# ScalarE fetches some token rows beside SyncE, and offsets are read 32 at a time

## The chip, the cores and the metric

The program runs on one core of one Trainium2 chip. A core has a matrix engine (TensorE, PE in the profile), two vector-like engines (VectorE, DVE; ScalarE, ACT), a general engine (GpSimd, POOL) and SyncE (SP), which only issues DMAs. Each has its own queue of instructions, worked through in order, and they wait for each other through semaphores. DMAs can be issued from SP, ACT and POOL. The metric is the device time of one execution in microseconds (us), lower being better; the median of three runs counts. One further execution was recorded by the hardware profiler, and all durations below come from that one.

## The reference

A batch of 16384 rows goes through a recommender network:

```python
tok = word_emb[token_idx].mean(axis=1)          # 32 tokens of a 50000 x 300 table
e1, e2, e3 = (emb_mh[k][mh_idx[k]].mean(axis=1) for k in (1, 2, 3))   # 20 indices each, 64 wide
o1, o2, o3, o4 = (emb_oh[k][oh_idx[k]] for k in (1, 2, 3, 4))         # one index each
emb = concatenate([tok, e1, e2, e3, o1, o2, o3, o4], axis=1)          # 748 wide
wide = sums of one weight per small index
h = relu(emb @ W1 + b1); h = relu(h @ W2 + b2); h = relu(h @ W3 + b3) # 1024, 512, 256
return sigmoid(h @ Wd + bd + wide)
```

What matters here is the first line: 16384 x 32 rows of 300 float32 (1200 bytes) are picked out of a table in HBM and added up, 32 for each batch row.

## The kernel before, in words

**Tiles.** The batch is cut into 128 tiles of 128 rows; a batch row lies on a partition.

**The tokens.** `tokens()` (L289 to L312) works through the tiles in groups of two tokens (`TOK_GROUP`). A token of a tile is one indirect DMA issued from POOL (L303): it reads 128 indices, one a partition, and fetches 128 rows of the table. Six buffers of two tokens (`TOK_BUFS`) are in rotation, and `add_up` (L275 to L287) adds a group into a running sum on DVE three groups later (L279, L281, L286). The 32nd token (`j == N_TOK - 1`) of some tiles is not gathered by POOL: if the tile stands in `fetched`, its rows are there already and the group has one indirect DMA fewer.

**The fetches.** Which tiles those are is set by the list `fetches`: tiles from 4 on with `t % 5` equal to 0, 2 or 4. For each, `load_column` (L317 to L322) loads the tile's 128 indices of that token into one partition with a DMA from SP, `column_offsets` (L324 to L330) turns them into byte offsets with two small DVE operations, and `fetch` (L332 to L350) reads the offsets into SP's registers, 16 at a time (`LOADS`, one TENSOR_LOAD, L338), and issues one DMA of 1200 bytes for each row from SP (L347). The rows go to one of two buffers of the pool `fetched`. A fetch is spread over 20 steps (`FETCH_STEPS`) and starts 24 steps (`FETCH_AHEAD`) before the step in which the tile's last group is added up; its column is loaded 4 steps ahead of that and converted 1 step ahead.

**The small tables.** The other embeddings are turned into products: for six batch rows a step, DVE makes one-hot vectors of the indices (`hot`, L406), ACT scales a part of them (L413), PE multiplies them to counts (`pc`, L424), ACT copies the counts out (`cnt`, L427), and a tile later PE multiplies the counts with the tables (`pg`, L459) and DVE adds the parts up (`g`, L449). The tables are split into three bfloat16 terms first (`convert_tables`), with the small constants `minus_count` and `zeros`, which nothing reads later.

**The layers.** Of three tiles together, PE transposes the features (L500), DVE copies them out (`x`, L504), PE runs the layers in float32 (L577, outputs L609), and ACT applies bias and ReLU (`h`, L588). SP stores the results (L621).

**The order.** The order on each engine is written out by hand: a loop over 1435 steps (11 a tile and 27 at the end) calls each of these pieces in turn, and each engine's queue holds them in that order. `tokens_by` gives how many groups the token stream should have made by a step (2 a step for 24 steps, then an even pace). Within a step the order is: one-hots and the scaling for the next step, eviction of earlier layer outputs, counts and their eviction, small sums, transposes, column loads and offsets, the rows of the fetches under way, the token groups, key columns, the layers, late small sums. `speed` sets how much of the layers is done in a step: one tile in 10.4 steps, in 8.5 near the end and in 6.0 (`TILE_STEPS_LAST`) in the last 14 steps. `load_indices` (L352 to L369) loads the indices of two tiles from SP: one DMA for the tokens (L357) and two for the small tables (L362).

**Semaphores of DMAs.** DMAs issued from SP and ACT share eight semaphores in rotation, in the order in which the program is written, and each DMA waits until the DMA eight before it, which had its semaphore, has landed. POOL's indirect DMAs have eight of their own.

Of the kernel before, what the change touches and what calls it, by code (L numbers as in the profile page):

```python
# [19 lines left out]
P = 128  # L20
N_TOK, TOK_D = 32, 300
N_MH, EMB = 20, 64
ROW = EMB + 1
# [3 lines left out]
TOK_BUFS = 6  # L27
HOT_BUFS = 2
FETCH_FROM = 4
FETCH_STEPS = 20  # L30
FETCH_AHEAD = 24
COLUMN_AHEAD = 4
COLUMN_LAG = 1
LOADS = 16
ROW_BYTES = 4 * TOK_D
WAKE = 27
EARLY = 3
BLOCK = 256
# [4 lines left out]
FRONT_PACE = 2.0  # L43
TILE_STEPS = 10.4
TILE_STEPS_SUMS = 8.5
TILE_STEPS_LAST = 6.0
STORE_LAG = 2
HALF = P // 2
UPPER = 256.0
# [23 lines left out]
IDX_MH = N_TOK  # L73
IDX_COLS = N_TOK + N_SMALL
# [3 lines left out]
def kernel(  # L78
# [21 lines left out]
    nc = tc.nc  # L100
    B = out.shape[0]
    NSUB, N = BLOCK // P, LAYER_TILES * P
# [5 lines left out]
    for f in SMALL:  # L108
        n = -(-tables[f].shape[0] // P)
# [4 lines left out]
    const = ctx.enter_context(tc.tile_pool(name="const", bufs=1))  # L114
# [3 lines left out]
    ohp = ctx.enter_context(tc.tile_pool(name="onehot", bufs=HOT_BUFS))  # L118
    cp = ctx.enter_context(tc.tile_pool(name="counts", bufs=2))
    fp = ctx.enter_context(tc.tile_pool(name="fetched", bufs=2))  # L120
    gp = ctx.enter_context(tc.tile_pool(name="g", bufs=3))
    wp = ctx.enter_context(tc.tile_pool(name="wide", bufs=2))
    xp = ctx.enter_context(tc.tile_pool(name="x", bufs=1))
# [51 lines left out]
    at = 0  # L175
# [2 lines left out]
        at += n  # L178

    terms = const.tile([P, n_h, 3 * ROW], BF16, name="terms")  # L180
    minus_count = const.tile([P, P], BF16, name="minus_count")
    nc.vector.tensor_single_scalar(minus_count, ident, -1.0 / COUNT, op=ALU.mult)

    zeros = const.tile([P, ROW], F32, name="zeros")
    nc.vector.memset(zeros, 0.0)

    def load_tables(part0, tag):
# [100 lines left out]
    def tokens():  # L288

        under_way = []  # L290
        for n in range(n_all):
            if n < n_all - TOK_LAG:
                t, q = divmod(n, n_groups)
                it = token_indices[t // NSUB][:, t % NSUB, :].bitcast(U32)
                tok_rows = tokp.tile([P, TOK_GROUP * TOK_D], F32, name="tok_rows")
                rows = []
                for r in range(TOK_GROUP):
                    j = q * TOK_GROUP + r
                    if j == N_TOK - 1 and t in fetched:
                        rows.append(fetched.pop(t))  # L300
                        continue
                    rows.append(tok_rows[:, r * TOK_D : (r + 1) * TOK_D])
                    nc.gpsimd.indirect_dma_start(  # L303
                        out=rows[-1],
                        out_offset=None,
                        in_=word,
                        in_offset=bass.IndirectOffsetOnAxis(ap=it[:, j : j + 1], axis=0),
                    )
                under_way.append((t, q, rows))
            if n >= TOK_LAG:  # L310
                add_up(*under_way.pop(0))
            yield 1  # L312

    fetched, columns = {}, {}
    word_bytes = word.bitcast(U8).rearrange("n d -> (n d)").unsqueeze(0)

    def load_column(t):  # L317

        columns[t] = fp.tile([1, P], I32, name="column")
        nc.sync.dma_start(  # L320
            out=columns[t], in_=idx[t * P : (t + 1) * P, N_TOK - 1 : N_TOK].rearrange("n o -> o n")
        )  # L322

    def column_offsets(t):  # L324


        column = columns[t]
        low = ROW_BYTES & -ROW_BYTES
        nc.vector.tensor_single_scalar(column, column, ROW_BYTES // low, op=ALU.mult)
        nc.vector.tensor_single_scalar(column, column, low.bit_length() - 1, op=ALU.logical_shift_left)  # L330

    def fetch(t):  # L332


        rows = fp.tile([P, TOK_D], F32, name="fetched").bitcast(U8)
        column = columns.pop(t)
        for p0 in range(0, P, LOADS):
            _, values = nc.values_load_multi_w_load_instructions(  # L338
                column[:, p0 : p0 + LOADS],
                engines=[mybir.EngineType.SP],  # L340
                min_val=0,
                max_val=(word.shape[0] - 1) * ROW_BYTES,
                skip_runtime_bounds_check_because="the indices are rows of the table",
            )
            for i, value in enumerate(values):
                p = p0 + i
                nc.sync.dma_start(out=rows[p : p + 1, :], in_=word_bytes[:, bass.ds(value, ROW_BYTES)])  # L347
                if p == P - 1:
                    fetched[t] = rows.bitcast(F32)
# [323 lines left out]
    tiles = B // P  # L673
# [40 lines left out]
    ix = load_indices(0)  # L714
# [8 lines left out]
    for step in range(n_steps):  # L723
        t, i = divmod(step, STEPS)
        s = t % NSUB
# [40 lines left out]
        for at, t_f in fetches:  # L766
            if step == at - COLUMN_AHEAD:
                load_column(t_f)
            if step == at - COLUMN_LAG:
                column_offsets(t_f)  # L770
            if step == at:
                fetching.append((at, Paced(fetch(t_f))))
        for at, rows in list(fetching):
            rows.to(P * (step + 1 - at) / FETCH_STEPS)
            if step + 1 - at >= FETCH_STEPS:
                rows.finish()
                fetching.remove((at, rows))
# [78 lines left out]
```

## Time and profile before

| what | value |
|---|---|
| time, median of three runs | 7247.27 us (7244.57 to 7274.91) |
| time of the profiled execution | 5068.49 us |
| its span, first to last instruction | 5066.7 us |
| mean granted TensorE clock | 0.982 |
| busy PE, DVE, ACT, POOL | 4811.1, 3748.8, 2739.9, 3807.6 us |
| indirect DMAs from POOL | 4021 |
| rows fetched by SP one by one | 9600 (75 tiles) |
| bytes moved by DMA | 653.52 MB, of these 617.88 MB by POOL's queue |

The span begins with the first instruction of the program and ends with the last; 1.8 us lie around it in the profiled execution. "Busy" counts the time in which an engine works on an instruction; issuing a DMA from SP or ACT, reading registers and waiting for semaphores are the sequencer's work and not in it. For POOL an indirect DMA is in it[...]. Of a line of the list of groups, the numbers after the bar are the busy time in all, the mean of one in ns, and the idle time of the engine just ahead of such instructions with what ended it. In the view of a tile's instructions the three numbers are the shortest, the median and the longest in ns, followed by the first and the last start in us. The time of the runs without the profiler is 1.43 times that of the profiled execution; the profile doesn't tell where the other 2178.8 us are.

### The profile page before, as it was taken

Reading aid. Unit: us, or ns where it says so; the run is one execution under the profiler, and the core shown is the slowest. Engines: PE = TensorE matmul, PEld = TensorE weight load, DVE = VectorE, ACT = ScalarE, POOL = GpSimd, SP = SyncE. Lnnn points to the kernel's source line nnn. Section 1 sums busy time; section 2 is a strip of 40 time slices with the busy share of each in tenths; the row PEclk is TensorE's granted clock in tenths of the full one; section 3 lists DMA queues with packets and bytes.
Section 4 is the critical chain, followed back from the end, with each engine's and each line's share of the span. In section 5 each row is a group of like instructions: output and inputs, shape, how many; then the busy total and the mean of one; then the engine's idle time right before and its main releaser. Section 6 shows DMA issues by size and latency. Waiting matters only on the chain.

```text
span 5066.7 us, 115364 instructions
## 1 busy us (share of the span) xinstructions
PE 4811.1 (95%) x36252; PEld 3731.2 (74%) x36252; DVE 3748.8 (74%) x6814; ACT 2739.9 (54%) x3658; POOL 3807.6 (75%) x4028
## 2 busy tenths in 40 slices
PE   6799999999999999999999999999999999999998
PEld 4577776677776777677777777767767888888898
DVE  6777777777777777777777777777777777777773
ACT  5455555555555555555555555555555555555552
POOL 7777777777777777777777777777777777777775
PEclk9899999999999999999999999999999999999999
DMA  7444444444444444444444444444444444444443
GB/s 203 127 128 128 128 128 128 128 128 128 127 128 129 127 128 128 128 129 127 128 128 127 128 128 126 128 129 127 128 128 127 128 129 128 128 128 127 129 127 97
DMA packets 280720, 653.52 MB, mean 129 GB/s; under 512 B 139419, under 2 KB 149659, under 8 KB 280103
## 3 DMA queue, kind: packets, MB, share of 16 engines
q0 software_dynamic: 193008, 617.88, 45.3%
q1 hardware_dynamic: 87095, 28.26, 2.7%
q8 instruction: 283, 4.64, 0.4%
q14 instruction: 334, 2.74, 0.2%
HBM read 645.63 MB, written 0.07 MB: 127 GB/s over the span
## 4 chain that ended last, share of the span: by engine, by line
PE 58%; DMA 14%; DVE 11%; issue 8%; POOL 4%; SPq 2%; ACT 1%; DVEq 0%; POOLq 0%; ACTq 0%
PE ph L577 31%; PE pg L459 20%; DMA tok_rows<-in_word_emb_dram,it 14%; PE pc L424 6%; POOL tok_rows L303 4%; DVE hot L406 4%; DVE own L286 3%; DVE own L281 2%; SPq L347 2%; PE pc L500 1%; DVE x L504 1%; ACT hot L413 1%; DVE g L449 1%; SPq L338 1%; ACT cnt L427 0%
## 5 line engine op out<-in xcount | busy, mean ns | idle before, releaser
L303 POOL DMA_INDIRECT tok_rows<-in_word_emb_dram,it x4021 | 3806.7, 947 | 1226.9 <-issue 784.0
L413 ACT ACTIVATE hot<-hot 64x768 bf16<-64x768 bf16 (+1 forms) x1408 | 1155.5, 821 | 1728.6 <-DVE hot L406 1717.0
L459 PE MATMUL pg<-terms,cnt 128*128 128x195 bf16 x17664 | 1723.6, 249 | 35.5 <-DVE g L449 35.5
L459 PEld LDWEIGHTS <-cnt 128*128 128x128 fp8e3 x17664 | 1529.0, 98 | 107.0 <-issue 80.1
L577 PE MATMUL ph<-x,w_sb 128*128 128x384 f32 (+5 forms) x4932 | 1506.4, 444 | 63.7 <-DVE x L504 53.6
L406 DVE TENSOR_TENSOR hot<-own,sc 128x1656 bf16<-128x1656 bf16 (+1 forms) x1408 | 1394.3, 990 | 213.3 <-PE pc L424 134.9
L427 ACT ACTIVATE cnt<-pc 128x828 uint16<-128x828 f32 (+1 forms) x1408 | 1187.5, 843 | 385.7 <-PE pc L424 367.5
L577 PE MATMUL ph<-h,w_sb 128*128 128x384 f32 (+2 forms) x4160 | 1221.7, 434 | 1.5 <-ACT h L588 1.5
L286 DVE TENSOR_TENSOR own<-own,tok_rows 128x300 f32<-128x300 f32 x1792 | 857.2, 478 | 377.2 <-DMA tok_rows<-in_word_emb_dram,it 327.2
L577 PEld LDWEIGHTS ph<-x,w_sb 128*128 128x128 f32 (+1 forms) x4932 | 846.1, 194 | 374.6 <-DVE x L504 62.9
L281 DVE TENSOR_TENSOR own<-own,tok_rows 128x300 f32<-128x300 f32 x1920 | 917.5, 478 | 233.5 <-DMA tok_rows<-in_word_emb_dram,it 178.3
L424 PEld LDWEIGHTS <-hot 128*128 128x128 bf16 x8192 | 592.5, 98 | 465.0 <-issue 201.0
L577 PEld LDWEIGHTS ph<-h,w_sb 128*128 128x128 f32 x4160 | 700.9, 191 | 250.5 <-ACT h L588 3.7
L424 PE MATMUL pc<-hot 128*128 128x138 bf16 x8192 | 729.5, 225 | 90.8 <-ACT hot L413 81.4
L588 ACT ACTIVATE h<-ph,b_sb 128x384 f32<-128x384 f32 (+2 forms) x723 | 379.1, 524 | 140.3 <-PE ph L577 125.6
L449 DVE TENSOR_REDUCE g<-pg 128x130 f32<-128x390 f32 (+1 forms) x512 | 259.8, 507 | 238.8 <-PE pg L459 236.7
L504 DVE TENSOR_TENSOR x<-pc,scale 128x768 f32<-128x768 f32 x127 | 120.9, 952 | 49.8 <-PE pc L500 49.0
L500 PE MATMUL pc<-ident,g 128*128 128x128 f32 x762 | 108.0, 279 | 9.8 <-ACT cnt L427 8.9
L393 DVE COPY sc<-pc 128x512 bf16<-128x512 bf16 x64 | 44.1, 689 | 81.5 <-PE pc L389 79.5
L279 DVE TENSOR_TENSOR own<-tok_rows 128x300 f32<-128x300 f32 x128 | 61.4, 480 | 47.2 <-DMA tok_rows<-in_word_emb_dram,it 44.2
L500 PEld LDWEIGHTS pc<-ident,g 128*128 128x128 f32 x762 | 84.1, 143 | 15.5 <-ACT cnt L427 14.3
L609 PE MATMUL po<-h,wd_sb 128*1 128x384 f32 (+2 forms) x208 | 70.6, 426 | 21.9 <-ACT h L588 20.7
(56 smaller groups left out, 436.6 us busy)
## 6 DMA issues: line engine op xcount, KB each, us to landing
fetched<-in_word_emb_dram SPq DMA_DIRECT2D x9600, 1.2 KB
tok_rows<-in_word_emb_dram,it POOLq DMA_INDIRECT x4021
ix<-in_idx_dram SPq DMA_DIRECT2D x128, 32.0 KB
w_sb<-in_W_dram SPq DMA_DIRECT2D x6, 512.0 KB
raw<-in_mh_dram SPq DMA_DIRECT2D x4, 682.5 KB
it<-in_idx_dram SPq DMA_DIRECT2D x64, 32.0 KB
w_sb<-in_W_dram SPq DMA_DIRECT2D x1, 2048.0 KB
column<-in_idx_dram SPq DMA_DIRECT2D x75, 0.5 KB
```

Of the source, the lines that this page charges most:

```text
L281: nc.vector.tensor_add(tok_sum, tok_sum, a)
L286: nc.vector.tensor_add(to, tok_sum, b)
L303: nc.gpsimd.indirect_dma_start(out=rows[-1], out_offset=None, in_=word, in_offset=bass.IndirectOffsetOnAxis(ap=it[:, j : j + 1], axis=0),)
L406: nc.vector.tensor_tensor(hot[:, 0 : 2 * rows, :].rearrange("p i (n d) -> p i n d", d=2), iota.rearrange("p (n d) -> p n d", d=2).unsqueez ...
L413: nc.scalar.activation(upper, upper, AF.Copy, scale=UPPER)
L424: nc.tensor.matmul(pc[:, k // n, at : at + n_h], hot[:, 2 * k, 0:P], hot[:, 2 * k + 1, :], start=True, stop=True)
L427: nc.scalar.activation(cnt[:, :, b : b + rows].rearrange("l h (g k) -> l h g k", g=2), pc[:, :, 0 : n * n_h].rearrange("l g (k h) -> l h g ...
L449: nc.vector.tensor_reduce(field_columns(features(t), pair), pg[:, 0:n, :].rearrange("p f (c d) -> p f d c", c=3), AX.X, ALU.add,)
L459: nc.tensor.matmul(pg[:, j, :], by_slice[:, h, :], terms[:, h, :], start=(h == h0), stop=(h == h1 - 1))
L500: nc.tensor.transpose(pt[:, j // n, j % n, :], g[:, c : c + P], ident)
L577: nc.tensor.matmul(to, weights[: src.shape[0], k, m * P : (m + 1) * P], src, start=(k == 0), stop=(k == len(srcs) - 1),)
L588: nc.scalar.activation(dst[:, m, 0:n], ph[:, 0:n], AF.Relu, bias=bias[:, m : m + 1])
```

## The change

SP now fetches the 32nd token of tiles from 4 on with `t % 3` equal to 1 or 2, spread over 16.5 steps that start 25 or 19.5 steps ahead. ACT fetches the 31st token (`N_TOK - 2`) of every fourth tile from tile 8 on, in the same manner, over 38 steps that start 42 steps ahead. TENSOR_LOADs read 32 offsets each instead of 16. ACT's rows have one buffer, in a new pool; the column of its offsets lies where `minus_count` and `zeros` were, in a common tile `early_use`. `load_indices` loads the small indices of two tiles with one DMA instead of two. In the last 14 steps the layers are done at one tile in 9 steps instead of 6. Line numbers of the new kernel are up to 5 higher in `tokens` and the groups after it, so that L303 becomes L308, L347 becomes L356, and L338 becomes L347.

```diff
-FETCH_STEPS = 20
-FETCH_AHEAD = 24
+FETCH_STEPS = 16.5
+FETCH_AHEAD = {1: 25.0, 2: 19.5}
+SCALAR_FROM, SCALAR_EVERY = 8, 4
+SCALAR_STEPS = 38.0
+SCALAR_AHEAD = 42.0
-LOADS = 16
+LOADS = 32
-TILE_STEPS_LAST = 6.0
+TILE_STEPS_LAST = 9.0
...
+    fa = ctx.enter_context(tc.tile_pool(name="fetched_scalar", bufs=1))
...
-    minus_count = const.tile([P, P], BF16, name="minus_count")
+    early_use = const.tile([P, P // 2 + ROW], I32, name="early_use")
+    minus_count = early_use[:, 0 : P // 2].bitcast(BF16)
...
-    zeros = const.tile([P, ROW], F32, name="zeros")
+    zeros = early_use[:, P // 2 : P // 2 + ROW].bitcast(F32)
...
-                    if j == N_TOK - 1 and t in fetched:
-                        rows.append(fetched.pop(t))
+                    if (t, j) in fetched:
+                        rows.append(fetched.pop((t, j)))
...
-    def load_column(t):
-        columns[t] = fp.tile([1, P], I32, name="column")
+    def load_column(t, j):
+        columns[t, j] = early_use[0:1, 0:P] if j < N_TOK - 1 else fp.tile([1, P], I32, name="column")
...
-    def fetch(t):
-        rows = fp.tile([P, TOK_D], F32, name="fetched").bitcast(U8)
-        column = columns.pop(t)
+    def fetch(t, j):
+        by_scalar = j < N_TOK - 1
+        rows = (fa if by_scalar else fp).tile([P, TOK_D], F32, name="fetched").bitcast(U8)
+        column = columns.pop((t, j))
+        queue, engine = (
+            (nc.scalar, mybir.EngineType.Activation) if by_scalar else (nc.sync, mybir.EngineType.SP)
+        )
         for p0 in range(0, P, LOADS):
...
-                engines=[mybir.EngineType.SP],
+                engines=[engine],
...
-                nc.sync.dma_start(out=rows[p : p + 1, :], in_=word_bytes[:, bass.ds(value, ROW_BYTES)])
+                queue.dma_start(out=rows[p : p + 1, :], in_=word_bytes[:, bass.ds(value, ROW_BYTES)])
...
-        for s in range(NSUB):
-            nc.sync.dma_start(
-                out=ix[s * HALF : (s + 1) * HALF],
-                in_=idx[b0 + s * P : b0 + (s + 1) * P, IDX_MH:IDX_COLS].rearrange(
-                    "(p f) c -> p f c", f=2
-                ),
-            )
+        nc.sync.dma_start(
+            out=ix, in_=idx[b0 : b0 + BLOCK, IDX_MH:IDX_COLS].rearrange("(p f) c -> p f c", f=2)
+        )
...
-    fetches = [(int(summed_at(t)) - FETCH_AHEAD, t) for t in range(FETCH_FROM, tiles) if t % 5 % 2 == 0]
+    fetches = [
+        (summed_at(t) - FETCH_AHEAD[t % 3], FETCH_STEPS, t, N_TOK - 1)
+        for t in range(FETCH_FROM, tiles)
+        if t % 3
+    ]
+    fetches += [
+        (summed_at(t) - SCALAR_AHEAD, SCALAR_STEPS, t, N_TOK - 2)
+        for t in range(SCALAR_FROM, tiles, SCALAR_EVERY)
+    ]
...
+        for at, n, *of in fetches:
+            if step == int(at) - COLUMN_AHEAD:
+                load_column(*of)
+            if step == int(at) - COLUMN_LAG:
+                column_offsets(*of)
+            if step == int(at):
+                fetching.append((at, n, Paced(fetch(*of))))
+        for entry in list(fetching):
+            at, n, rows = entry
+            rows.to(P * (step + 1 - at) / n)
+            if step + 1 - at >= n:
+                rows.finish()
+                fetching.remove(entry)
```

More of the change, by code (lines that the diff above doesn't have):

```diff
@@ L315, with column_offsets @@
     word_bytes = word.bitcast(U8).rearrange("n d -> (n d)").unsqueeze(0)
-    def load_column(t):
-        columns[t] = fp.tile([1, P], I32, name="column")
+    def load_column(t, j):
+        columns[t, j] = early_use[0:1, 0:P] if j < N_TOK - 1 else fp.tile([1, P], I32, name="column")
         nc.sync.dma_start(
-            out=columns[t], in_=idx[t * P : (t + 1) * P, N_TOK - 1 : N_TOK].rearrange("n o -> o n")
+            out=columns[t, j], in_=idx[t * P : (t + 1) * P, j : j + 1].rearrange("n o -> o n")
         )
-    def column_offsets(t):
-        column = columns[t]
+    def column_offsets(t, j):
+        column = columns[t, j]
         low = ROW_BYTES & -ROW_BYTES
@@ L346, in fetch @@
                 p = p0 + i
-                nc.sync.dma_start(out=rows[p : p + 1, :], in_=word_bytes[:, bass.ds(value, ROW_BYTES)])
+                queue.dma_start(out=rows[p : p + 1, :], in_=word_bytes[:, bass.ds(value, ROW_BYTES)])
                 if p == P - 1:
-                    fetched[t] = rows.bitcast(F32)
+                    fetched[t, j] = rows.bitcast(F32)
                 yield 1
@@ L765 @@
             layers, target = start(block), 0
[L766 to L775, printed above, removed]
+        for at, n, *of in fetches:
[9 more added lines that the diff above has]
+            if step + 1 - at >= n:
                 rows.finish()
-                fetching.remove((at, rows))
+                fetching.remove(entry)
         toks.to(tokens_by(step + 1))
```

## The prediction

> **What bounds the kernel now.** I read the groups of the page first, then the instructions of the token tile, then the waits, then a long stretch in the middle.
>
> ```profile
> PE 4811.1 (95%) x36252; PEld 3731.2 (74%) x36252; DVE 3748.8 (74%) x6814; ACT 2739.9 (54%) x3658; POOL 3807.6 (75%) x4028
> ...
> q0 software_dynamic: 193008, 617.88, 45.3%
> q1 hardware_dynamic: 87095, 28.26, 2.7%
> ```
>
> By busy time PE looks like the bound (95%) and POOL far from it (75%). The next view, the instructions of the token tile, says otherwise:
>
> ```profile
> L303 POOL DMA_INDIRECT tok_rows<-in_word_emb_dram,it x4021: 942/946/1372, 3.0 to 5034.2; - x192
> ```
>
> The 4021 gathers start between 3.0 and 5034.2 us, so they follow each other every 5031.2 / 4020 = 1.2515 us on average, while one takes 0.946 us. What lies between two of them is in the waits:
>
> ```profile
> POOL tok_rows L303 <- issue: 784.0, 2572, 0.3
> ...
> DVE own L286 <- DMA tok_rows<-in_word_emb_dram,it: 327.2, 509, 2.9
> ...
> DVE own L281 <- DMA tok_rows<-in_word_emb_dram,it: 178.3, 247, 3.1
> ...
> PEld L424 <- ACT hot L413: 115.6, 92, 5.2
> PE pc L424 <- ACT hot L413: 81.4, 60, 4.5
> ```
>
> POOL's longest gap is 0.3 us, the same as its mean (784.0 / 2572): a fixed price of one gather, not a wait for anybody. In the trace's records only 25 of the 4020 distances are over 1.3 us, and these add 4.6 us together. So POOL never waits for a buffer, for indices or for another engine, from the first gather to the last, and the adders on DVE wait for it. The stretch from 1000 to 4000 us (us, then busy time of PE, PEld, DVE, ACT and POOL) shows how close PE follows:
>
> ```profile
> 1000.00:4000.00 3000.00, 2888.89 (x21144) 2147.83 (x21142) 2260.42 (x4091) 1636.11 (x2121) 2269.50 (x2397) 0.99 0.48 128
> ```
>
> PE is busy 96.3% and has 3.7% left. After the last gather at 5034.2 the span has 32.5 us to go: the adds, a transpose and the layers of the last tile. So the time is 4021 gathers x 1.2515 us, 3 us ahead and 32 us behind.
>
> **What the Trainium skill says.** "DMA: Bandwidth & Descriptors", section "Issuing engines are not separate DMA queues", says that DMAs of all issuers run on the same 16 engines, so that another issuer saves issue time alone. Here issue time is what is short: the queues above fill 45.3% and 2.7% of the 16 engines. "Perfetto Trace Analysis", section "Per-instruction lifecycle", says that a DMA from such a queue is worked off by the sequencer, with the descriptor generator locked while it is used, whereas an engine's instruction is pushed into a queue, so that the sequencer is free again. The trace agrees half: in 19 of 27 cases a semaphore wait of ACT's own sequencer runs while the ACTIVATE in front of it is still busy (the one at 4037.345 us, the wait at 4037.353), but no sequencer work of ACT is seen ahead of that start. I take it that row DMAs run beside the ACTIVATE in front of them and not beside a wait.
>
> **The change part by part.** The profiled execution is the base (5068.49 us, span 5066.7).
>
> *Fewer gathers.* Before, 75 tiles have their last token from SP. After, the tiles from 4 to 127 that 3 doesn't divide are 83, and the tiles 8, 12, ... 124 are 30 for ACT: 113 gathers are left out instead of 75, 38 more. POOL makes 3983, and 38 x 1.2515 = 47.6 us go from the path that sets the end. Bounds: 0, if another engine is the bound then, and 47.6. I take 47.6, since PE would be at 96.3 x 1.0095 = 97.2% in the middle, below full, and PE's remaining waits come mostly from DVE work that is held up by late gathers.
>
> *SP's rows.* The prices:
>
> ```profile
> L338 SPq TENSOR_LOAD <-column x600: 1132/1232/1493, 116.2 to 5011.0; - x150
> ```
>
> ```profile
> 2424.89 5.10 SPq L347 DMA_DIRECT2D fetched<-in_word_emb_dram  x16
> ```
>
> Sixteen rows take 5.10 us, 0.320 each; 16 offsets 1.232 us, 1.28 with what lies around. A fetch was 128 x 0.320 + 8 x 1.28 = 51.2 us. The same DMA page, section "Latency and other measured facts", gives a load into registers a floor of about 0.6 us; with it 16 offsets cost 0.6 + 16 x 0.0395, and 32 are estimated at 1.86, say 1.92 with what lies around (bounds 1.28 and 2.56; no run here shows it). A fetch becomes 41.0 + 4 x 1.92 = 48.6 us. SP's fetches go from 75 x 51.2 = 3840 to 83 x 48.6 = 4034 us. POOL needs 3983 / 128 x 3 x 1.2515 = 116.8 us for three tiles; SP's two fetches are 97.2 and its other DMAs some 4, so it keeps up: +194 us of SP, nothing on the path.
>
> *ACT's rows.* 30 fetches: 3840 DMAs and 120 loads, 3840 x 0.320 + 120 x 1.92 = 1229 + 230 = 1459 us of ACT's sequencer, spread over 30 x 38 = 1140 steps: 3.4 rows or 1.08 us a step. They stand behind the counts' copy (L427, 0.861 us), and in front of the next `hot` (L413), for which PE waits. The 0.861 us cover most of the 1.08; 0.22 us a step, and 1.06 us at a load, are left. ACT waits (1717.0 for L406 + 367.5 for L424 + 125.6 for L577) / 1435 = 1.54 us a step, so I cost this at nothing; without that cover it is 1140 x 0.22 + 120 x 1.06 = 378 us in ACT's order, the upper bound. A gain is excluded, since nothing leaves ACT.
>
> *Shared semaphores.* Rows on ACT wait for the DMA eight earlier, mostly SP's; `hot` is queued behind, and PE behind that. SP's rows were issued at a steady 0.320 us with the same wait, so eight rows (2.56 us) were enough for a landing. 8 to 11 rows a step of 3.5 us are no faster. Cost 0, up to one landing of 2.5 us at the 30 starts of a fetch (75 us).
>
> *The small rest.* 38 more pairs of offset operations on DVE (L329, L330: 0.204 + 0.216) are 16 us on an engine that is idle for a quarter; one DMA of indices fewer for each pair of tiles takes 64 x 0.584 = 37 us from SP, 38 more columns at 0.577 add 22; both hidden. The slower pace in the last 14 steps moves at most 14 x (1/6 - 1/9) = 0.8 of a tile's layers (21 us a tile at the end of the trace), 16 us, behind; in the order that the program is built to, only two output chunks of some 1 us each pass the early part of the last block, and PE waits 6.85 us there. I take 0, between -5 and +16.
>
> *Sum.* 5068.5 - 47.6 = 5020.9 us in the profiled execution. The runs are 1.430 times longer than that, for a reason that the page doesn't show. If what paces the program is slower in them in proportion, a gather costs 1.79 us and 38 of them 68 us: 7179. If the difference is a constant outside the program: 7200. I take the first, as POOL's gathers fill the span and a constant of 2179 us has no trace in the 1.8 us around it: **7180**, with 7165 to 7205 for this case.
>
> **The rivals.** *Another bound in the runs (no change).* The runs may be 1.43 times longer because PE, not POOL, is slower there; 38 gathers fewer are then worth nothing, ACT's rows fall into its waits: 7247, between 7225 and 7265. For it: PE has only 3.7% of room in the trace. Against it: the granted clock is 0.99 there.
>
> *ScalarE's issuing reaches PE (slower).* Place: between L427 and the next L413. Price: the 378 us above, of which a third, 126 us, reaches PE. PE's idle 255.6 us (5066.7 - 4811.1) would keep 208 after the gain, and the new ones come on top: 5066.7 - 47.6 + 126 = 5145, +78; times 1.43, 7360. It decides from 47.6 us on, an eighth of the 378. For it: PE already waits 197 us for L413. Against it: 1.54 us of waits a step, and one-hots are made a step ahead.
>
> *SP falls behind (slower).* If a load of 32 costs over 3.8 us, two fetches and the rest pass 116.8 us; at 4.2 they are 119.7, for 42.7 times three tiles 5111, and about 7310. Twice the price of 16 is 2.56, so this is unlikely.
>
> **How the numbers follow.** Forecast 0.66; no change 0.16; ScalarE 0.13; SP 0.05. Half a per cent, 36 us, is about what a measurement of this kernel can tell from no change. Faster takes nearly all of the first case: 0.65; same 0.17; slower 0.18. The range must leave out 0.2 at most: 7160 to 7290 holds the first two cases, with a margin for a small part of ACT's cost.
>
> **What would show it.** Right: 3983 gathers, still 1.25 us apart and with no gap over 0.3, the last near 4987, the span near 5019; DVE still waiting for `tok_rows`; a load of 32 between 1.3 and 2.6 us; PE's waits for L413 (now L418) no more than today's 197 us. ScalarE's rival would show in these waits, and in gaps of POOL that end with DVE. SP's rival would show as DVE waiting for `fetched` (12.5 us today). Wrong altogether: a span as I say with runs that don't follow it, which would put the bound of the runs outside what this trace shows.

## The result and the profile after

The kernel after takes 8189.33 us (median of 6 runs, 8176.83 to 8193.95), the kernel before in the same runs 7268.47 us (7244.57 to 7286.02): a ratio of 1.1263, 95% interval 1.1241 to 1.1284. That is 921 us slower, where 68 us faster was forecast. The profiled execution of after took 8191.97 us, which agrees with its runs. Lines of its page, of the token tile, of the stretch from 1000 to 4000 us and of its waits (engine, what waited, for whom: us in all, times, longest):

```profile
span 8190.0 us, 125163 instructions
...
PE 5746.5 (70%) x36252; PEld 4189.8 (51%) x36252; DVE 3776.3 (46%) x6890; ACT 2742.6 (33%) x3658; POOL 3770.9 (46%) x3990
...
q0 software_dynamic: 191184, 612.04, 27.7%
q1 hardware_dynamic: 93591, 29.51, 1.8%
q10 hardware_dynamic: 7680, 4.62, 0.3%
```

```profile
L308 POOL DMA_INDIRECT tok_rows<-in_word_emb_dram,it x3983: 940/947/1242, 3.0 to 8143.1; - x200
```

```profile
1000.00:4000.00 3000.00, 2116.36 (x12938) 1472.93 (x12935) 1399.82 (x2544) 1005.57 (x1299) 1382.71 (x1461) 0.84 0.30 79
```

```profile
POOL tok_rows L308 <- DVE own L291: 2738.7, 577, 26.8
...
DVE column L334 <- DMA column<-in_idx_dram: 884.9, 77, 22.9
PEld L429 <- ACT hot L418: 736.4, 205, 19.1
...
PE pc L429 <- ACT hot L418: 609.0, 158, 18.5
```

The new queue q10 holds ScalarE's rows, and no queue is near full. PE was busy 96% of the middle stretch and is now at 71%. POOL makes the 3983 gathers that were forecast, but it waits 2739 us for DVE; in the profile of before it never waited for anybody. DVE waits 885 us for columns of indices (2 us in the profile of before), and the wait of PE's weight loads for L418 (L413 before) grew from 116 to 736 us. The matmuls' own wait for the same line, 81 and 609 us, runs at the same time: together they cover 116 and 738 us, so the 197 us of the prediction, their sum, counts most of it twice.

Two things are mixed in this. The kernel before itself takes about 7280 us on some chips and about 5070 on others; its profiled execution (5068.49) was of the second kind, its timed runs of the first. I call the kinds *7280* and *5070*. Each chip was used at one time only, so nothing here shows whether the kind belongs to the chip or to the hour. Every ratio below is to runs of the kernel before on the same chip; both kernels were profiled on both kinds. On a *5070* chip the change costs 948 us as well, and its trace is the easier one to read. Waits of the kernel after there:

```profile
ACT hot L418 <- DVE hot L411: 2102.8, 923, 22.3
POOL tok_rows L308 <- DVE own L291: 985.0, 395, 20.3
DVE column L334 <- DMA column<-in_idx_dram: 906.1, 81, 22.8
...
PEld L429 <- ACT hot L418: 659.2, 171, 18.6
PE pc L429 <- ACT hot L418: 537.3, 126, 17.5
```

And SP's own waits, by the same columns, first in the profile of before (L338 is the load of offsets, which comes first in a fetch and so waits for a free buffer), then in that execution of after (L347 is that load, L356 the row):

```profile
SPq L338 <- DVE own L286: 664.0, 66, 27.5
...
SPq L338 <- DVE own L281: 25.3, 4, 18.1
SPq L338 <- DVE x L616: 20.3, 1, 20.3
...
SPq L338 <- DVE g L449: 17.1, 4, 5.2
```

```profile
SPq L356 <- DMA fetched<-in_word_emb_dram: 1369.4, 1431, 17.2
...
SPq L347 <- DVE own L291: 38.9, 19, 11.1
```

In the profile of before, SP waited 727 us for DVE to free its buffers and had no wait for a landing of its rows in the list: it was ahead of its work. Now 125 us of the first are left (39 in the longest line), and it waits 1369 us for rows to land. What that does to the others is seen in one stretch (start, length, engine, line; in brackets the idle time ahead and who ended it):

```profile
2999.79 5.86 SPq L356 DMA_DIRECT2D fetched<-in_word_emb_dram  x19
...
3005.75 0.58 SPq L325 DMA_DIRECT2D column<-in_idx_dram  x1
...
3007.99 0.21 DVE L334 TENSOR_SCALAR column<-column 1x128 int32<-1x128 int32 x1 [13.31 <-DMA column<-in_idx_dram]
...
3009.62 0.94 POOL L308 DMA_INDIRECT tok_rows<-in_word_emb_dram,it  x1 [11.70 <-DVE own L291]
...
3010.68 1.63 PE L464 MATMUL pg<-terms,cnt 128*128 128x195 bf16 x9 [10.40 <-DVE g L454]
```

SP is still issuing rows when DVE has come to the column that stands behind them in SP's queue. DVE stands still for 13.3 us, and POOL and PE behind it for 11.7 and 10.4. The chain of work that ended last shows how SP came to be late (start, length, what; "DMA" is the time from an issue to its landing):

```profile
2989.88 2.00 DMA fetched<-in_word_emb_dram
2991.89 0.21 ACTq L356
...
2995.35 0.63 ACT cnt L432
2996.01 0.71 ACT hot L418
2996.75 1.77 DMA fetched<-in_word_emb_dram
2998.54 0.22 SPq L356
...
3005.75 2.14 DMA column<-in_idx_dram
3007.99 0.23 DVE column L334
```

The row that SP issued at 2989.88 has to land before ScalarE can issue the next one on its semaphore (2991.89). ScalarE's row of 2996.75 stands behind two activations, and SP's row at 2998.54 waits until that one has landed. 22 more rows follow, and then the column that DVE waits for.

### The profile page after: what moved, and what is told of

The parts are those of the page before. It is cut to its first block, busy times and chain, and to the rows that moved or that the text cites. A ratio compares the mean times of both kernels' runs of the same rounds, so it can differ in the third digit from the quotient of the medians.

```text
span 8190.0 us, 125163 instructions
## 1 busy us (share of the span) xinstructions
PE 5746.5 (70%) x36252; PEld 4189.8 (51%) x36252; DVE 3776.3 (46%) x6890; ACT 2742.6 (33%) x3658; POOL 3770.9 (46%) x3990
## 5 line engine op out<-in xcount | busy, mean ns | idle before, releaser
L308 POOL DMA_INDIRECT tok_rows<-in_word_emb_dram,it x3983 | 3770.0, 947 | 4372.6 <-DVE own L291 2738.7
L464 PE MATMUL pg<-terms,cnt 128*128 128x195 bf16 x17664 | 2083.9, 270 | 813.9 <-issue 524.2
L464 PEld LDWEIGHTS <-cnt 128*128 128x128 fp8e3 x17664 | 1713.2, 107 | 1034.1 <-issue 974.0
L418 ACT ACTIVATE hot<-hot 64x768 bf16<-64x768 bf16 (+1 forms) x1408 | 1155.2, 820 | 2963.8 <-DVE hot L411 2194.4
L582 PE MATMUL ph<-x,w_sb 128*128 128x384 f32 (+5 forms) x4932 | 1718.0, 490 | 270.2 <-ACT h L593 110.4
L582 PE MATMUL ph<-h,w_sb 128*128 128x384 f32 (+2 forms) x4160 | 1390.6, 476 | 146.5 <-ACT h L593 86.9
L429 PE MATMUL pc<-hot 128*128 128x138 bf16 x8192 | 834.4, 243 | 852.8 <-ACT hot L418 609.0
L429 PEld LDWEIGHTS <-hot 128*128 128x128 bf16 x8192 | 654.9, 107 | 1378.9 <-ACT hot L418 736.4
L582 PEld LDWEIGHTS ph<-x,w_sb 128*128 128x128 f32 (+1 forms) x4932 | 951.3, 217 | 663.8 <-issue 183.4
L582 PEld LDWEIGHTS ph<-h,w_sb 128*128 128x128 f32 x4160 | 783.5, 212 | 472.1 <-issue 159.8
L291 DVE TENSOR_TENSOR g<-own,fetched 128x300 f32<-128x300 f32 x83 | 39.0, 470 | 331.2 <-DMA fetched<-in_word_emb_dram 319.9
```

The source lines that it names most:

```text
L291: nc.vector.tensor_add(to, tok_sum, b)
L308: nc.gpsimd.indirect_dma_start(out=rows[-1], out_offset=None, in_=word, in_offset=bass.IndirectOffsetOnAxis(ap=it[:, j : j + 1], axis=0),)
L418: nc.scalar.activation(upper, upper, AF.Copy, scale=UPPER)
L429: nc.tensor.matmul(pc[:, k // n, at : at + n_h], hot[:, 2 * k, 0:P], hot[:, 2 * k + 1, :], start=True, stop=True)
L464: nc.tensor.matmul(pg[:, j, :], by_slice[:, h, :], terms[:, h, :], start=(h == h0), stop=(h == h1 - 1))
L582: nc.tensor.matmul(to, weights[: src.shape[0], k, m * P : (m + 1) * P], src, start=(k == 0), stop=(k == len(srcs) - 1),)
```

## The experiments

Two theories stood against each other. **A, coupling:** rows of SP and of ScalarE use eight completion semaphores in turn; SP stands behind rows that ScalarE issues only between its activations, loses its lead and becomes the bound. **B, own time:** ScalarE's 3840 rows and their loads delay ScalarE's activations, and so PE, whatever SP does. A third, **C**, was that only the columns come too late.

| kernel | *7280* chips | *5070* chips |
|---|---|---|
| before | 7268 to 7284 | 5067 to 5072 |
| no fetch at all | 7044.5 | 5158.0 |
| ScalarE's fetches alone | 7122.8 | 5121.4 |
| SP's share of the change alone | 7282.4 | not run |
| before, with ScalarE's fetches | 7956.6 | 5679.9 |
| after | 8189.3 | 6015.1 |

**The kernel before once more.**

> The kernel before, unchanged, to see what its runs are made of: its profiled execution took 5068.5 us and its six runs about 7268, while the changed kernel's profile and runs agree at 8190. Theory (SP's sequencer has a slow mode, in which each of its instructions takes about 0.7 us): the runs of the kernel before have slow stretches as well, and a profile at 7268 shows MOVE and row DMAs of 0.7 us on SP, as the changed kernel's does, and DVE waiting for column or fetched. Rival (the clock): a profile at 7268 shows SP at its usual 0.32 us a row and all of PE's instructions longer. Rival (a chance profile): the profile is at 5068 again and the runs as well.

7279.67 us (20 runs), 1.0005 (0.9991 to 1.0019). Its profiled execution has a span of 7278.4, and it is a *7280* one. The tile that SP fetches (shortest, median and longest instruction in ns), first in the profile ahead of the prediction, then here:

```profile
L347 SPq MOVE fetched<-in_word_emb_dram x9600: 29/29/43, 117.4 to 5017.0; - x196
```

```profile
L347 SPq MOVE fetched<-in_word_emb_dram x9600: 2/29/1398, 153.3 to 7232.8; - x196
```

And its waits:

```profile
POOL tok_rows L303 <- DVE own L286: 2042.8, 594, 10.2
...
PEld L459 <- issue: 944.4, 969, 12.0
```

The same program, instruction for instruction. On a *5070* chip no MOVE of SP is longer than 43 ns; here 1440 are over 100 ns, in stretches in which SP gets on by one instruction in about 0.7 us (or 1.4), row DMAs included. PE does it too: in one such stretch of SP, from 3020 to 3026 us, its weight loads start from 3022 on at 3022.10, 3022.21, 3022.83, 3023.55, 3024.26, 3024.96 and 3025.68. A single start is not exact there: 787 of the 9600 rows have their bytes moving before the start that the trace gives their instruction (none in the profile of before). The waits of PE's weight loads for nothing that the profile shows ("issue", L459) are 944 us against 80. So POOL, which never waited in the profile of before, waits 2043 us for DVE here: the bound of the runs isn't the bound of that profile. The rival that the clock stretches all of PE's work is not borne out: the granted clock is 0.877 here against 0.982, but the median matmul of the table products takes 248 ns in both.

**SP's share alone**: the kernel after without ScalarE's fetches.

```diff
-    fetches += [
-        (summed_at(t) - SCALAR_AHEAD, SCALAR_STEPS, t, N_TOK - 2)
-        for t in range(SCALAR_FROM, tiles, SCALAR_EVERY)
-    ]
```

> The changed kernel without ScalarE's fetches; POOL gathers those 30 tokens (4013 gathers, 83 tiles by SP with 32 offsets a load). Theory A (ScalarE's rows, coupled with SP's through the eight shared semaphores and the shared issuing, make the loss): back to 7268 or below, 7200 to 7300. Theory B (SP is asked for more than it can do, by 83 tiles at an even rate and loads of 32): most of the loss stays, 7900 to 8200. POOL alone would give 8 gathers fewer, 10 to 15 us.

7282.42 us, 0.9999 (0.9982 to 1.0017). The new tiles, the even pace, the loads of 32, the merged load of indices and the slower end cost nothing together as long as ScalarE fetches nothing, and gain nothing. Beside ScalarE's fetches this isn't so (next run).

**ScalarE's fetches added to the kernel before**, with its 75 tiles of SP and loads of 16: `fetch`, `load_column` and the merged load of indices as in after, and to the list of before

```diff
+    fetches += [
+        (summed_at(t) - SCALAR_AHEAD, SCALAR_STEPS, t, N_TOK - 2)
+        for t in range(SCALAR_FROM, tiles, SCALAR_EVERY)
+    ]
```

> The kernel before with ScalarE's fetches added (30 tiles), SP's own 75 tiles, 16 offsets a load and the pace of the last steps as before. Theory A (ScalarE's rows): about the changed kernel's time, 7900 to 8200. Theory B (SP overloaded by its own tiles and loads): near the kernel before, 7200 to 7350.

7956.57 us, 1.0937 (1.0907 to 1.0967): 679 of the 921 us by which after was slower than before. The rest comes only with SP's share of the change on top, which alone cost nothing; on *5070* chips it is 336 of 948 (below). Which part of SP's share does it wasn't tried.

**Loads of 32 in the kernel before.**

```diff
-LOADS = 16
+LOADS = 32
```

> The kernel before with loads of 32 offsets and nothing else. In the changed kernel such a load takes 2.12 us where 16 take 1.23, so 4 take 8.5 us where 8 took 9.9. Theory A: no change, 7230 to 7290. Theory B: slower by some per cent if it is the loads that hold SP up.

7257.23 us, 0.9976 (0.9965 to 0.9987): 0.2% faster. The longer loads alone aren't the cause.

**No fetch** in the kernel before.

```diff
-    fetches = [(int(summed_at(t)) - FETCH_AHEAD, t) for t in range(FETCH_FROM, tiles) if t % 5 % 2 == 0]
+    fetches = []
```

> The kernel before, without any row by row fetch: all 4096 gathers are made by POOL. If POOL's gathers at 1.25 us each set the time of the runs, 75 more cost 94 us: 7370. If something outside POOL sets it (in the profile of the repeated kernel before, POOL stands idle for 3426 us and waits for DVE in 2043 of them), the time stays within 40 us of 7277. If SP's 9600 row fetches themselves slow the other engines, it falls, to 7150 or less.

7044.52 us, 0.9674 (0.9654 to 0.9693): with 75 gathers more, it is 239 us faster. On a *7280* chip gathers are not the bound, and SP's fetches cost time there. With them gone SP has 661 instructions instead of 20669, and PE's wait at L459 for nothing shown falls from 944 to 712 us. This version beats both kernels on such chips. It also shows that the rows are not what makes such a chip slow in the main: without any of them the kernel takes 7045 us there, against 5158 on a *5070* chip (last run).

**ScalarE's fetches alone**: the run with them added, without SP's.

```diff
-    fetches = [
-        (int(summed_at(t)) - FETCH_AHEAD, FETCH_STEPS, t, N_TOK - 1)
...
+    fetches = []
     fetches += [
```

> ScalarE's 30 fetches as in the run with them added, and none by SP. Theory A, coupling: ScalarE's rows are dear because each waits for the DMA eight earlier on shared semaphores, mostly one of SP's, and SP crawls in stretches. Without SP's rows they wait for ScalarE's own earlier rows alone, so the time is within 150 us of the kernel without fetches: 7250 to 7430. Theory B, ScalarE's own time: 3840 rows at 0.213 us and 120 loads at 2.23 us are 1086 us of its sequencer ahead of the activations, whatever SP does; then the time stays near 7957, above 7800.

7122.80 us: 78 more than without any fetch, although POOL makes 30 gathers fewer. SP's fetches cost 239 and ScalarE's 78, but both together 912 (7956.57 against 7044.52, on two chips on which before differs by 6 us): some 595 us appear only when the two engines fetch side by side. That speaks for A and against B.

**Columns 12 steps ahead** in the kernel after.

```diff
-COLUMN_AHEAD = 4
+COLUMN_AHEAD = {True: 5, False: 12}
...
-            if step == int(at) - COLUMN_AHEAD:
+            if step == int(at) - COLUMN_AHEAD[of[1] < N_TOK - 1]:
```

> The kernel after, with the column of indices of each SP fetch loaded 12 steps ahead instead of 4 (ScalarE's 5 instead of 4). Theory C, late columns: the kernel after loses its last 233 us against the run with only ScalarE's fetches added because DVE waits 885 us in the profile for these columns, queued on SP behind rows; with them loaded earlier the wait falls below 300 us and the time to 7900 to 8000. If the columns are late only because SP itself is late by more than 12 steps, or another wait takes over, it stays at 8100 to 8190.

8196.01 us, 1.1251 (1.1230 to 1.1272), as after. In its waits DVE's wait for SP's columns is down to 5 us, and its wait for SP's rows has grown from 320 us to this:

```profile
DVE g L291 <- DMA fetched<-in_word_emb_dram: 920.7, 55, 34.5
```

The wait has moved from the columns (885 us in after) to the rows; the two together fell from 1205 to 926 us, and the time did not. SP as a whole is late, and C falls.

**Fixed rows**: the run with ScalarE's fetches added; ScalarE's rows all copy row 0 of the table, without its register loads.

```diff
+            if by_scalar:
+                values = [0] * LOADS
+            else:
...
+                row = word_bytes[:, 0:ROW_BYTES] if by_scalar else word_bytes[:, bass.ds(value, ROW_BYTES)]
```

> The run with ScalarE's fetches added, but ScalarE's rows all copy the first row of the table (so the sums are of other rows), and its 120 register loads are gone; SP's part, the number of DMAs and their semaphores are the same. Theory A, coupling: the loads are a small part; 7957 less at most 120, so 7830 to 7960. Theory B, ScalarE's own time: 120 loads at 2.23 us are 268 of 1086 us of its sequencer, and the longest pieces; a quarter to a half of the 679 us goes, 7620 to 7790.

8228.12 us, 1.1298 (1.1277 to 1.1319), which is 271 us slower than with the loads. Neither theory expected that. SP's waits for rows to land rose from 1436 to 1850 us, so the sign is that of A, but why they rose isn't settled. That all rows now come from one place is not the reason: from ScalarE's issue to the last byte a row takes 1.08 us in the median with the loads and 1.10 here. What it does show is that ScalarE's loads (240 with 16 offsets each in these runs, not the 120 of the expectations) aren't what costs.

**Separate semaphores, first try.** Whose semaphore a row gets is set by the count of DMAs so far, so ScalarE's rows are put among SP's by that count, five of SP and three of ScalarE in turn. In `fetch`, ahead of a row of SP:

```diff
+                while not by_scalar and scalar_rows and dmas[0] % 8 in (5, 6, 7):
+                    if next(scalar_rows[0], None) is None:
+                        scalar_rows.pop(0)
```

The control has `dmas[0] % 16 in (2, 3, 4, 13, 14, 15)` there.

> The run with ScalarE's fetches added, with ScalarE's rows put among SP's so that they fall on three of the eight completion semaphores and SP's on the other five (five rows of SP, three of ScalarE, in turn): an SP row stands behind a row of ScalarE on the same semaphore 136 times instead of 2699. The same rows, loads and bytes. Theory A, coupling: SP no longer waits for rows that ScalarE issues between its activations; what is left is the price of ScalarE's rows alone, 78 us, on about 7280: 7300 to 7480. Theory B, ScalarE's or the DMA engines' load: the work is the same and in tighter lumps of three, so 7850 or more.

> The control of the run with separate semaphores: the same five and three rows in turn, in the same order on every engine, with the lumps of ScalarE shifted so that each row of ScalarE takes a semaphore that SP used last, and SP stands behind ScalarE 3834 times. Theory A: at least as slow as the run with ScalarE's fetches added, 7950 to 8500. Theory B: the same as the run with separate semaphores, within 60 us.

> The kernel after with separate semaphores for the two engines' rows, as in the other run of that kind. Theory A: SP's share of the change costs nothing and ScalarE's rows 78 us, so 7330 to 7500; then the whole loss of 912 us but for some 100 was the sharing. Theory B: near 8190.

6374.73 (separate), 6658.59 (control) and 6340.24 us (after, separate), on a *5070* chip: 1.2571, 1.3125 and 1.2490 times the kernel before. These three tell little. The order of ScalarE's queue had been left free, and its rows slipped past activations, so that up to 63, 66 and 39 of them lay between two, where the kernel after has at most 4; in one place of the trace ScalarE issues rows from 4713 to 4751 us with no activation between. The statement in the second expectation that the order is the same on every engine was wrong.

**Half of ScalarE's fetches** in the run with them added.

```diff
-SCALAR_FROM, SCALAR_EVERY = 8, 4
+SCALAR_FROM, SCALAR_EVERY = 8, 8
```

> The run with ScalarE's fetches added, but only for every eighth tile, 15 fetches instead of 30; an SP row stands behind ScalarE 1327 times. If every shared row costs a fixed amount, half of the 679 us is left: 7620. If SP has room of its own first (it waits for buffers for over 800 us in the repeated kernel before) and becomes the bound only when that is used up, less than half: 7350 to 7550.

5355.20 us, 1.0556 (1.0539 to 1.0574): 283 us, against 612 for all 30 on another *5070* chip (below). So 46% of the loss for half of the fetches, nearer the first of the two outcomes than the second: there is no free room that has to be used up first. SP still waits 352 us for free buffers in that run, in the line for `own`, and the 283 us are lost all the same.

**Separate semaphores, in order.** As above, with the instructions of SP and of ScalarE tied to the order of the program again, each behind the one before it; and two runs repeated beside it, unchanged.

> Separate semaphores again (five rows of SP, three of ScalarE in turn, an SP row behind a row of ScalarE 136 times instead of 2699), and now each engine's instructions in the order in which the program was written, so that at most nine rows of ScalarE lie between two of its activations (in the first try up to 63 did). Theory A, the shared semaphores tie the two engines: the loss against the kernel before is less than half of that of the run with ScalarE's fetches added on the same chip. Theory B, ScalarE's rows cost their own time, or the two queues hinder each other elsewhere: the loss is the same within a fifth, since rows and loads are the same.

> The control: five and three in turn as well, but with ScalarE's lumps shifted so that SP stands behind ScalarE 3834 times; SP's order is the same, at most twelve rows of ScalarE lie between two activations. Theory A: a loss at least as large as that of the run with ScalarE's fetches added. Theory B: the same as with separate semaphores, within a tenth of the loss.

> The run with ScalarE's fetches added, unchanged, on the chip of the other three. If this chip runs the kernel before in about 7280 us, 7957 again; if in about 5072, and SP is the bound there too (9600 rows at 0.32, 600 loads at 1.24 and a wait for ScalarE at 2700 of them), 5700 to 6200.

> ScalarE's fetches alone, unchanged, on the same chip. Theory A: no SP rows to be tied to, so a small loss: about 7120 where the kernel before takes 7280; where it takes 5072, POOL's 4066 gathers at 1.2515 us set the time, 5089 + 35 = 5124, up to 5180. Theory B: ScalarE's own 1086 us of issuing show in full where PE has 4% of room: 5400 or more on such a chip.

All four ran on one *5070* chip, with the kernel before at 5067.94:

| kernel | us | ratio and interval | SP behind ScalarE | SP waits for landings, us | of these for ScalarE's rows | ScalarE's `hot` waits for landings | DVE waits for SP's columns and rows |
|---|---|---|---|---|---|---|---|
| ScalarE alone | 5121.41 | 1.0105 (1.0089 to 1.0122) | – | – | – | 130 | – |
| separate | 5354.78 | 1.0563 (1.0546 to 1.0581) | 136 DMAs | 527.2 | 94 | 696 | 9 |
| control | 5514.47 | 1.0881 (1.0863 to 1.0899) | 3834 | 839.2 | 780 | 1008 | 7 |
| ScalarE's added | 5679.85 | 1.1205 (1.1186 to 1.1223) | 2701 | 1276.1 | 1206 | 293 | 778 |

The sixth column is counted from the traces: the time over the usual 0.320 us from row to row, for rows over 0.36 us behind the row ahead, where the DMA eight earlier was ScalarE's and only a register move lies between. It is measured otherwise than the fifth, so the two are close and not to be subtracted.

ScalarE's fetches alone show no cost of their own on such a chip. Its gathers, in the view of the tile:

```profile
L308 POOL DMA_INDIRECT tok_rows<-in_word_emb_dram,it x4066: 942/946/1204, 3.0 to 5088.0; - x194
```

4066 gathers x 1.2515 + 35 us = 5124; measured 5121. B falls. With SP's rows beside them the loss is 612 us, and with the same rows on separate semaphores 287: 325 less, and 160 less than the control, in which SP's queue is the same and only the places of ScalarE's rows are shifted. The control by itself is 166 us faster than the run with ScalarE's added, so of the 325 only these 160 are shown for the semaphores themselves. SP has its lead back in the separate run, and ScalarE has a wait of its own instead:

```profile
SPq L359 <- DVE own L303: 458.6, 60, 19.3
```

```profile
ACT hot L433 <- DMA fetched<-in_word_emb_dram: 696.0, 275, 12.7
```

(L433 is L418 of after.) Its lumps, mostly of three to nine rows between two activations, now turn round in three semaphores, and the fourth row of a lump waits for the landing of the first. I take this for the source of the 287 us that are left; separating the semaphores without that (with more of them) wasn't tried.

The control lost less than the run with ScalarE's added, against the expectation, though SP stands behind ScalarE at more DMAs. The table shows that it stands there but waits less: 780 us against 1206 (648 in the half run, with a loss of 283), and DVE waits for SP's columns and rows 7 us against 778. So in the run with ScalarE's added, as in after (1213 us, and 1075 of DVE), the loss goes through SP to DVE; in the control and the separate run DVE hardly waits for SP, and what the waits show instead is ScalarE's activations, which wait for landings. No simple sum of these waits gives the four losses. Nor does the count of lumps in the programs: 1160 where ScalarE's are added, 768 in the control, 580 in the half, which is 0.53, 0.58 and 0.49 us for each, but after has the same 1160 and loses 0.82 for each.

**After and no fetch on a *5070* chip.**

> The kernel after, unchanged, once more. Where the kernel before takes about 7280 us: 8190 again. Where it takes about 5070: SP has 10624 rows (0.32 us, 3400 us) and 332 loads (about 2.0, 660 us) and stands behind ScalarE at 2664 of the rows, with 0.4 us more for each of these than for the others in the run with ScalarE's fetches added (0.855 against 0.466), about 1050 us; 5700 to 5900, although 38 gathers fewer leave POOL 4985 us of work. The forecast's own sum for such a chip was 5021.

> The kernel before without any fetch, 4096 gathers, once more. Where the kernel before takes about 7280 us: 7045 again, 3.3% less. Where it takes about 5070, POOL's gathers set the time: 4096 at 1.2515 and 35 us around them, 5161, 1.8% more.

After: 6015.13 us, 1.1867 (1.1847 to 1.1887), more than I expected. No fetch: 5157.95, 1.0180 (1.0163 to 1.0197), where 5161 was worked out. The same edit is 3.3% faster on one kind of chip and 1.8% slower on the other, since on this one POOL is the bound, as the profile ahead of the prediction had it.

## Why the prediction was wrong, point by point

**What bounds the kernel.** Right for the profile, wrong for the runs. On *5070* chips POOL's price of 1.2515 us a gather holds to 3 us in 5100, twice (4066 and 4096 gathers). In an execution like the timed runs POOL waits 2043 us for DVE, and 75 gathers more came with a shorter time. The step that carried the sum over, "If what paces the program is slower in them in proportion, a gather costs 1.79 us", failed: a gather takes 946 ns in both kinds, and POOL waits. The other 2180 us lie inside the program, where SP and PE have stretches of one instruction in 0.7 us; but without SP's rows most of the difference stays (7045 against 5158), and its cause is open. The first rival, another bound in the runs, had this half right. This step is not what made the forecast miss: the change costs 948 us on *5070* chips too, where the sum of the prediction, 5020.9, needs no such step.

**Fewer gathers.** The count was right. They gained nothing on either kind of chip: on *7280* chips POOL wasn't the bound, and on *5070* chips it no longer was.

**SP's rows.** A load of 32 was estimated at 1.92 us with what lies around it; the load alone takes 2.13 in the profile on the *5070* chip (2.12 on the other), inside the bounds of 1.28 to 2.56 but over the estimate. The two measured loads lie on a line that starts at 0.34 us without any offset, not at the 0.6 taken from the skill's floor:

```profile
L347 SPq TENSOR_LOAD <-column x332: 2037/2129/2354, 112.9 to 5958.6; - x166
```

"SP keeps up" held for SP's share alone (0.9999, on *7280* chips). Its margin can be worked out from the forecast's own numbers: 116.8 - 97.2 - 4 = 15.6 us for three tiles, 666 us over 42.7 of them; in the profile of before, where it had 194 us less to do, SP waited 727 us for buffers. The forecast never compared this room with anything.

**ScalarE's rows.** "I cost this at nothing" held where ScalarE fetches alone on a *5070* chip: 5121 us is the time of the gathers. On *7280* chips the price was 78 us net of 30 gathers fewer, below the 378 of the upper bound.

**Shared semaphores: the step that failed.** It said "Cost 0, up to one landing of 2.5 us at the 30 starts of a fetch (75 us)", because 8 to 11 rows in a step of 3.5 us are no faster than rows 0.320 us apart. That compares mean rates. SP doesn't issue its eight rows at the mean rate but as fast as it can, and among them stands one that ScalarE issues when its activations let it. Counted in the trace of after on the *5070* chip: where the DMA eight earlier was SP's, a DMA of SP follows SP's DMA ahead of it after 0.437 us on average (8293 times), and where it was ScalarE's after 0.900 (2654 times). That is 0.463 x 2654 = 1229 us in place of 75. It isn't slow landing: from issue to landing an SP row takes 1.72 us in the median and 2.73 at most there, in the profile of before 1.78 and 2.42. ScalarE's row is issued too late for SP's place in the order. In the 1281 cases in which an SP row with only a register move ahead of it came late (over 0.36 us after the row ahead) behind a row of ScalarE, it started 0.57 us (median) after the last byte of that row had come.

These 1229 us can't be set against the room of 666 to give the loss: in the half run SP waits 648 us for ScalarE's rows, less than the 727 of its room in before, and 283 are lost. SP loses its lead while ScalarE fetches and has it again later, when nobody needs it; that is how I read it, and no run shows it.

"DMA: Bandwidth & Descriptors", section "Anatomy of one DMA — SWDGE (gpsimd) path", of the Trainium skill says that "any semaphore wait happens on the issuing sequencer before dispatch". The section is about DMAs from GpSimd; the trace agrees for those of SP and ScalarE: the wait stands in SP's queue, with the next column behind it, and in ScalarE's (354 us before activations in after on the *5070* chip). The same page, which I had used for the view that a further issuing engine saves issue time alone, advises under "Why a DMA increments its semaphore by 16 and not by 1": "One semaphore per in-flight slot, not one per stream." It says so against reading data that has not landed yet, which can't happen here, since each DMA waits for the one before it on its semaphore; that slots shared by two streams cost time is what the runs show. Taking them apart gave back 160 us against the control, and 325 with the other arrangement of the rows, of 612. A rival is the granted clock, which fell from 0.982 to 0.916: PE is busy 189 us longer in after (5000.5 against 4811.1), but it is idle for 1020 us and the median matmul of the table products takes 248 ns in both, so it can't be the main cause.

**The rivals.** The time went to the side of "ScalarE's issuing reaches PE", and the sign named for it appeared: PE's waits for L418 rose from 197 to 1196 us on the *5070* chip, by the prediction's way of adding, and POOL has gaps that end with DVE. But the mechanism was wrong: ScalarE's issuing costs nothing there without SP's rows. The sign of the third rival, DVE waiting for `fetched`, appeared as well (12.5 us before; 168.5, and 906 for columns). It was SP that fell behind, not by dear loads but by waits. The weight of 0.05 went to the rival that came nearest, for a reason that did not come true.

## What to carry to other kernels

Before work is given to a second issuing engine, look at which semaphores its DMAs share and with whom: an engine that issues freely inherits the timetable of one that issues between its computations, and the cost falls on its lead. The time that it waits for free buffers is no store against this: half of the shared waits, 648 us against 727 of such time, still cost 283 us. If a profile and the timed runs differ by 43%, the profile can show another bound than the runs have; repeat it before taking prices from it. When a wait is removed and the time stays, as with the columns here, look for the same microseconds further down the list.

## What the runs showed of the hardware

The same program took 5067 to 5072 us on three chips and 7277 to 7284 on two. On the latter, SP and PE have stretches of one instruction in about 0.7 us: in the repeated kernel before, 1440 MOVEs of SP over 100 ns and 945 row DMAs over 500 ns; none on the former. Why isn't shown. A gather takes 946 ns in the median on both. A load of 16 offsets into registers takes 1.23 us and one of 32 takes 2.13, some 0.056 us for each further offset. A row DMA takes 0.213 us of ScalarE's sequencer and 0.225 of SP's, and its row has landed 1.72 us (ScalarE's 1.85) after its start, in the median of after on a *5070* chip. DMAs of SP and of ScalarE that take turns on the same semaphores wait for each other in both queues, as the chain above shows.
